# Attention over a sparse graph: pairs of row tiles that share one gather slot, and a new order of the instructions

## The chip, the cores and the metric

The kernel runs on one core of a Trainium2 chip. The metric is the device time of one launch in microseconds (us), the median of several runs. One profiled execution, taken by the hardware profiler, gives the rows that are quoted below; its clock begins at its first instruction.

## What is computed

Sixteen batches of 1024 rows of 512 numbers each; one adjacency matrix for all of them, in which row *i* has a one at each neighbour (itself among them).

```python
# x: (16, 1024, 512), adj: (1024, 1024), Wq, Wk, Wv: (512, 512)
h = jnp.maximum(_layernorm(x, axis=-1), 0.0)
q = (h @ Wq + bq).reshape(b, n, 8, 64)          # k and v alike
scores = jnp.einsum('bihd,bjhd->bhij', q, k) / jnp.sqrt(jnp.float32(64))
scores = scores + jnp.where(adj == 0, -1e9, 0.0)
weights = jax.nn.softmax(scores, axis=-1)
out = x + jnp.einsum('bhij,bjhd->bihd', weights, v).reshape(b, n, 512)
```

The number of neighbours differs much from row to row: a few rows have many, most have one to four. The kernel works with lists of neighbours and never forms the 1024 x 1024 scores.

## The kernel before

**Tiles, slots, units.** The rows are sorted by their number of neighbours and cut into eight tiles of 128 rows, tile 0 with the longest lists. `CAPS` = (11, 8, 6, 5, 4, 3, 3, 2) says how many neighbours a row of tile 0, 1, ..., 7 gets. A *slot* is one neighbour for each of the 128 rows of a tile: K and V of that neighbour, 128 x 1024 numbers, 512 KB. Together with a unit of 4 slots (tile "-1") for rows of tile 0 whose list is longer still, a batch has 46 slots. They are grouped into 14 *units* (`PARTS`: tile, first slot, count). A slot that a row does not need still is fetched and worked on (it points to a spare row, and its weight is taken out of the sums).

**The work of a batch.** PE projects K and V of the batch (`proj_kv`), tile by tile, from the transposed normalized rows (`flip` on PE, `unflip` copies them out on ACT); ACT or DVE takes K and V out of PSUM (`evict_kv`), SP stores them to DRAM (`store_kv`). When all eight tiles are stored, POOL fetches the slots with an indirect DMA each (`gather`); a tile's own rows come by a plain DMA on SP. The slots lie in a ring of `RING` = 23. Then for each unit: DVE multiplies K with the queries (`multiply`, line 1360, the queries lie in a PSUM bank), DVE sums over the 64 columns of each head (`score`, L1364), ACT takes exponents (`exponent`, L1368), ACT multiplies V by the weights, eight small instructions for a slot (`weigh_s`, L1394), or DVE with one (`weigh_v`, L1380), and DVE or POOL add the slots of the unit together (`fold`, L1399; `join`, L1406, adds one unit to another). Tile 0 and the pieces of long rows are added by PE (`add_up`, L1418). DVE forms the sums of weights (`row_sums`, `more`), POOL or DVE adds the result to x and POOL writes it out by an indirect DMA.

**Overlap.** PE projects K and V of batch *b*+1 while DVE, ACT and POOL work on the units of batch *b*; the queries of batch *b* (`queries`, names `pq_<batch>_<tile>`) are projected in between. Before batch 0 the program loads the adjacency matrix, sums it, ranks the rows by a comparison of keys (`keys`, `rank_of`, `ranks`), and builds the lists; K and V of batch 0 are projected meanwhile from x in its given order (names with `_first`).

**What sets the order.** Every engine runs its instructions in program order. That order comes from `PLACES`, a table of one number for each step of a batch (`PERIOD` is added for each batch): `Plan.ordered` sorts the steps of each engine by this number and holds a step back only until what it needs has been issued and its buffer is free in the order of `POOLS`. PSUM gives two banks to the queries (`'q': 2`), two to K and V, two to the transposes and two to the sums. So the queries of a tile can begin only after the multiplications with the queries two tiles earlier.

## Time and profile before

| | |
|---|---|
| three runs | 1610.32, 1606.07, 1604.77 us; median 1606.07 us |
| span of the profiled execution, first to last instruction | 1595.8 us (the median is 10.3 us above it) |
| busy | PE 97%, its weight loads 45%, DVE 96%, ACT 90%, POOL 79% |
| DMA | 531.55 MB in the whole span |
| phases | 0 to 95 us: lists, and K and V of batch 0; then units; K and V of the last batch end at 1496.8 us; end 1595.8 us |

The time of the profiled execution is not listed apart from its span; what lies around the span is taken as the 10.3 us between it and the median of the runs. A share of the span is an average over the phases; the rows below therefore cut the span into stretches of 100 us.

### The profile page before, as it was taken

How to read it: one execution, taken by the hardware profiler on the slowest of the kernel's cores; microseconds unless marked ns; L12 is line 12 of the kernel's file. 1: busy time of each engine (PE TensorE's matmuls, PEld its weight loads, DVE VectorE, ACT ScalarE, POOL GpSimd, SP SyncE). 2: the span in 40 equal slices, each digit the busy share in tenths (PEclk: the TensorE clock that was granted, in tenths of full speed). 3: DMA queues.
4: the chain of work that ended last, by engine and by line, in shares of the span. 5: the costliest groups of instructions: out<-in, count | busy, mean ns of one | idle time of the engine just before them, and what ended most of it. 6: DMA issues, size and time to landing. Idle time of an engine off the chain costs nothing.

```text
span 1595.8 us, 19282 instructions
## 1 busy us (share of the span) xinstructions
PE 1548.5 (97%) x4151; PEld 719.2 (45%) x4182; DVE 1532.9 (96%) x2105; ACT 1437.5 (90%) x5428; POOL 1257.0 (79%) x1185
## 2 busy tenths in 40 slices
PE   8999999999999999999999999999999999999877
PEld 4444444444444444444444444444444444444333
DVE  8879999999999999999999999999999999999997
ACT  4359989889999999999999999999999998998997
POOL 3767788887888888888888888888888878876775
PEclk9999999999999999999999999999999999999989
DMA  6498989998999999999999999999999999988994
GB/s 251 141 356 308 323 331 347 343 344 323 320 376 340 371 333 337 344 346 375 335 354 343 352 340 342 373 347 372 326 357 339 342 368 328 364 338 295 333 376 191
DMA packets 149875, 531.55 MB, mean 333 GB/s; under 512 B 19052, under 2 KB 19052, under 8 KB 149752
## 3 DMA queue, kind: packets, MB, share of 16 engines
q0 software_dynamic: 109840, 390.70, 67.2%
q1 hardware_dynamic: 39912, 139.56, 23.7%
q8 instruction: 35, 0.57, 0.1%
q14 instruction: 88, 0.72, 0.1%
HBM read 429.46 MB, written 100.72 MB: 332 GB/s over the span
## 4 chain that ended last, share of the span: by engine, by line
DVE 39%; PE 22%; ACT 12%; POOL 10%; issue 9%; DMA 7%; DVEq 0%; POOLq 0%; SPq 0%; ACTq 0%
DVE ring L1360 11%; DVE weights L1364 10%; ACT ring L1394 9%; DVE ring L1399 6%; DMA ring<-kv,index 6%; PE pk L1117 5%; PE pv L1117 5%; PE pq L1117 5%; POOL ring L1350 4%; DVE ring L1380 3%; DVE st L1071 2%; PE pv_first L1117 2%; PE pk_first L1117 2%; POOL ring L1399 2%; POOL x L1062 1%
## 5 line engine op out<-in xcount | busy, mean ns | idle before, releaser
L1394 ACT ACTIVATE ring<-ring,weights 128x64 f32<-128x64 f32 x4704 | 1154.6, 343 | 43.4 <-DVE weights L1373 42.4
L1350 POOL DMA_INDIRECT ring<-kv,index x608 | 618.0, 1016 | 185.5 <-issue 159.7
L1117 PE MATMUL pq<-wq,hT 128*128 128x512 f32 x1024 | 460.3, 592 | 0.8
L1117 PE MATMUL pv<-wv,hT 128*128 128x512 f32 x960 | 433.2, 594 | 3.5 <-ACT kvt L1135 3.3
L1117 PE MATMUL pk<-wk,hT 128*128 128x512 f32 x960 | 433.2, 594 | 1.9 <-ACT hT L1109 1.2
L1364 DVE TENSOR_REDUCE weights<-ring 128x32 f32<-128x2048 f32 (+2 forms) x224 | 422.2, 1890 | 0.9
L1360 DVE TENSOR_TENSOR ring<-ring,pq 128x1536 f32<-128x1536 f32 (+2 forms) x208 | 388.7, 1869 | 4.6 <-DMA ring<-kv,index 4.0
L1117 PEld LDWEIGHTS pq<-wq,hT 128*128 128x128 f32 x1024 | 194.5, 190 | 215.0 <-issue 211.1
L1117 PEld LDWEIGHTS pv<-wv,hT 128*128 128x128 f32 x960 | 182.1, 191 | 227.1 <-issue 216.4
L1117 PEld LDWEIGHTS pk<-wk,hT 128*128 128x128 f32 x960 | 182.7, 191 | 211.0 <-issue 200.6
L1399 DVE TENSOR_TENSOR ring<-ring 128x512 f32<-128x512 f32 (+1 forms) x301 | 253.0, 856 | 2.7 <-ACT ring L1394 2.1
L1471 POOL DMA_INDIRECT out_dram<-x,perm x128 | 151.3, 1182 | 38.1 <-issue 24.4
L1062 POOL DMA_INDIRECT x<-in_x_dram,perm x128 | 142.3, 1111 | 34.0 <-issue 27.6
L1399 POOL TENSOR_TENSOR ring<-ring 128x512 f32<-128x512 f32 x90 | 116.1, 1299 | 10.0 <-DVE ring L1399 8.3
L1380 DVE TENSOR_TENSOR ring<-ring,weights 128x512 f32<-128x512 f32 x143 | 105.8, 747 | 1.3 <-ACT weights L1368 1.0
L1097 ACT ACTIVATE h<-x,shift,rstd 128x512 f32<-128x512 f32 x120 | 94.0, 814 | 0.9 <-DVE shift L1087 0.9
L1468 POOL TENSOR_TENSOR x<-x,o 128x512 f32<-128x512 f32 x64 | 82.4, 1288 | 15.3 <-DVE o L1454 12.7
L1104 PEld LDWEIGHTS pht<-ident,h 128*128 128x128 f32 x512 | 61.9, 141 | 55.6 <-issue 47.8
L1368 ACT ACTIVATE weights<-weights 128x32 f32<-128x32 f32 (+2 forms) x224 | 48.8, 223 | 42.0 <-DVE weights L1364 41.2
L1071 DVE BATCH_NORM_STATS2 st<-x 128x6 f32<-128x512 f32 x120 | 81.2, 677 | 0.1
L1135 ACT COPY kvt<-pk 128x512 f32<-128x512 f32 x120 | 69.4, 578 | 7.8 <-PE pk L1117 7.8
L1104 PE MATMUL pht<-ident,h 128*128 128x128 f32 x512 | 72.7, 274 | 2.7 <-ACT h L1097 2.7
(240 smaller groups left out, 1088.0 us busy)
## 6 DMA issues: line engine op xcount, KB each, us to landing
ring<-kv SPq DMA_DIRECT2D x128, 512.0 KB, 6.7
kv<-kvt SPq DMA_DIRECT2D x120, 512.0 KB, 6.5
ring<-kv,index POOLq DMA_INDIRECT x608, 7.0
ring<-in_adj_dram SPq DMA_DIRECT2D x8, 512.0 KB, 8.2
x_first<-in_x_dram SPq DMA_DIRECT2D x8, 256.0 KB, 6.0
x<-in_x_dram,perm POOLq DMA_INDIRECT x128, 6.1
out_dram<-x,perm POOLq DMA_INDIRECT x128, 5.8
wk<-in_L_gnn_Wk_dram SPq DMA_DIRECT2D x1, 1024.0 KB
```

What stands on the lines that cost most here:

```text
L1062: nc.gpsimd.indirect_dma_start(out=X[n][:], out_offset=None, in_=x_rows, in_offset=on(ap=perm[:, t : t + 1], axis=0), element_offset=b * N * D
L1071: nc.vector.bn_stats(st, X[n])
L1097: nc.scalar.activation(HN[n], X[n], AF.Relu, bias=shift, scale=scale)
L1104: nc.tensor.transpose(PH[n][:, c, :], hn[:, ts(c, P)], ident)
L1117: nc.tensor.matmul(pt, HT[n][:, c, :], W[name][:, c, :], start=(apart and c == 0), stop=(n != -NT and c == DC - 1))
L1350: nc.gpsimd.indirect_dma_start(out=G[i][:, s].rearrange("p j d -> p (j d)"), out_offset=None, in_=KV[b % len(KV)][:], in_offset=on(ap=inde ...
L1360: nc.vector.tensor_tensor(k, k, Q[b, t][:, None, :].to_broadcast([P, count, D]), ALU.mult)
L1364: nc.vector.tensor_reduce(weights[:, w, :], heads(G[i][:, :count, 0, :]), AX.X, ALU.add)
L1380: nc.vector.tensor_tensor(v, v, own.to_broadcast([P, n, H, HD]), ALU.mult)
L1394: nc.scalar.activation(v[:, h, :], v[:, h, :], AF.Identity, scale=weights[:, c + s, h : h + 1])
L1399: engine.tensor_tensor(v[:, 0:n], v[:, 0:n], v[:, first : first + n], ALU.add)
L1471: nc.gpsimd.indirect_dma_start(out=out_rows[t], out_offset=on(ap=perm[:, t : t + 1], axis=0), in_=X.pop(b * NT + TILES.index(t))[:], in_of ...
```

## The change

Tiles 2 and 3 give up their own last slot and share one: rows 0 to 63 of the shared slot serve the last neighbour of tile 2's rows, rows 64 to 127 that of tile 3's. Tiles 0 and 1 do the same, with rows 0 to 95 for tile 0 and rows 96 to 127 for tile 1. For this the rows of tiles 3 and 1 lie in reverse order in their tile, so that their longest lists stand at the high rows. A batch has 44 slots and 13 units; the ring has 22.

A shared slot needs a tile of mixed queries (`mix`, two copies on ACT for each pair: rows from one bank and from the other; the copy of tile 0's queries that was there, `copy_q`, is one of them), a multiplication of its own (`multiply_m`), a split of its weights (`halves`, two small copies on ACT), and two additions, one for each side (`fold_m` and `join_m` on DVE; in the last batch `add_m` on PE). `ranks` gets seven more small DVE instructions, which turn the order of tiles 1 and 3. Which slots DVE weighs is now written for each unit; nine per batch, as before. All numbers of `PLACES` are new.

```diff
-    3: ((3, 0, 3), (3, 3, 2)),
-    2: ((2, 0, 3), (2, 3, 3)),
+    3: ((3, 0, 5),),
+    2: ((2, 0, 3), (2, 3, 2)),
     1: ((1, 0, 4), (1, 4, 4)),
-    0: ((0, 0, 4), (-1, 0, 4), (0, 4, 4), (0, 8, 3)),
+    0: ((0, 0, 4), (-1, 0, 4), (0, 4, 4), (0, 8, 2)),
 }
+SHARED = {3: (2, 64), 1: (0, 96)}
...
-BY_VECTOR = {2: 1, 3: 0, 4: 1}
-ONE_MORE = ((2, 0),)
+BY_VECTOR = {(7, 0): 1, (4, 0): 1, (3, 0): 1, (2, 3): 1, (1, 0): 1, (1, 4): 1, (0, 0): 1, (-1, 0): 1, (0, 4): 1}
...
-PERIOD = 95.290021
+PERIOD = 93.3
...
-        queries=(102.781, 109.589, 125.334, 130.63, 135.829, 151.822, 160.48, 186.198, 199.518,),
+        queries=(104.758, 106.455, 110.927, 120.802, 128.186, 137.177, 154.399, 157.941, 178.55,),
...
-POOLS = {'x': 16, 'h': 2, 'pht': 2, 'hT': 11, 'pkv': 2, 'kvt': 4, 'q': 2, 'q0': 1, 'acc': 2, 'o': 1}
-RING = 23
+POOLS = {'x': 16, 'h': 2, 'pht': 2, 'hT': 11, 'pkv': 2, 'kvt': 4, 'q': 2, 'q0': 1, 'qm': 1, 'acc': 2, 'o': 1}
+RING = 22
...
+                elif t in SHARED or t in LOW:
+                    add(("mix", b, t), "ACT", [("queries", b, t)], [q, mixed(b, t)])
...
+            add(("multiply_m", k), "DVE", [slots[m], of_low, ("mix", b, t)], [mixed(b, t)])
+            add(("score", k), "DVE", [("multiply", k), ("multiply_m", k)])
...
+            nc.vector.scalar_tensor_tensor(mirror, tile_of, float(P), rank, op0=ALU.mult, op1=ALU.subtract)
...
+            nc.vector.tensor_tensor(rank, rank, mirror, ALU.add)
+            nc.vector.tensor_copy(rank_i, rank)
...
+            rows = dict(sides(high))[t]
+            nc.scalar.copy(QM[b, high][rows, :], Q[b, t][rows, :])
...
+        def multiply_m(i):
+            k = GM[i][:, 0, :]
+            nc.vector.tensor_tensor(k, k, QM[i // NU, UNITS[i % NU][0]], ALU.mult)
+
+        def halves(i):
+            high = UNITS[i % NU][0]
+            for t, rows in sides(high):
+                nc.scalar.copy(weights[rows, part_col[t], :], weights[rows, shared_col[high], :])
...
+        def fold_m(i):
+            rows = sides(UNITS[i % NU][0])[1][1]
+            v = G[i][rows, 0, 1, :]
+            nc.vector.tensor_tensor(v, v, GM[i][rows, 1, :], ALU.add)
+
+        def join_m(i):
+            low, rows = sides(UNITS[i % NU][0])[0]
+            v = G[i // NU * NU + parts_of(low)[0]][rows, 0, 1, :]
+            nc.vector.tensor_tensor(v, v, GM.pop(i)[rows, 1, :], ALU.add)
```

Counted over the whole program, gathers fall from 608 to 576 and the small weighing instructions of ACT from 4704 to 4448. On DVE the multiplications of 1536 columns go from 96 to 64, those of 1024 from 32 to 48, 32 of 512 are new, and the additions of 512 columns (`fold` and `join` before, with `fold_m` and `join_m` after) go from 286 to 271. On POOL the folds go from 90 to 105. PE's multiplications are the same in number but for one. The numbers of `PLACES` move instructions in three places that matter below.

SP, first instructions of the program, before (loads of x, of the biases, of the weights and of blocks of the adjacency matrix; `ring` is where biases and adjacency land):

```order
L1060 DMA x_first_0_151<-in_x_dram 128x512
L1060 DMA x_first_1_168<-in_x_dram 128x512
L951 DMA ring_104<-in_L0_gnn_bk_dram 3x512
L951 DMA ring_104<-in_L0_gnn_bv_dram 3x512
L951 DMA ring_104<-in_L0_gnn_bq_dram 3x512
L938 DMA wk_111<-in_L0_gnn_Wk_dram 128x4x512
L935 DMA ring_104<-in_adj_dram 128x1024
```

and after, at the same place:

```order
L1054 DMA ring_107<-in_adj_dram 128x1024
L1190 DMA x_first_2_163<-in_x_dram 128x512
L1070 DMA ring_107<-in_L0_gnn_bv_dram 3x512
L1190 DMA x_first_1_166<-in_x_dram 128x512
L1190 DMA x_first_0_170<-in_x_dram 128x512
L1054 DMA ring_107<-in_adj_dram 128x1024
L1070 DMA ring_107<-in_L0_gnn_bq_dram 3x512
L1057 DMA wk_114<-in_L0_gnn_Wk_dram 128x4x512
L1070 DMA ring_107<-in_L0_gnn_bk_dram 3x512
```

The weights of K, which stood behind two tiles of x (0.5 MB), now stand behind three tiles of x and two blocks of the adjacency matrix (1.75 MB).

PE, queries of tiles 4, 3 and 2 of batch 8, before (`chosen` adds the bias, `pk_9_5` is a projection of the next batch, `pht` a transpose):

```order
L1115 MATMUL pq_8_4_7388<-bias_parts_141,chosen_121 128x512
L1117 MATMUL pq_8_4_7388<-wq_113,hT_8_4_6583 128x512 x4
L1115 LDWEIGHTS chosen_121
L1115 MATMUL pq_8_3_7434<-bias_parts_141,chosen_121 128x512
L1117 MATMUL pq_8_3_7434<-wq_113,hT_8_3_6757 128x512 x4
L1115 LDWEIGHTS chosen_121
L1115 MATMUL pk_9_5_7466<-bias_parts_141,chosen_121 128x512
L1117 MATMUL pk_9_5_7466<-wk_111,hT_9_5_7380 128x512 x4
L1104 MATMUL pht_9_3_7476<-ident_114,h_9_3_7384 128x128 x4
L1115 LDWEIGHTS chosen_121
L1115 MATMUL pq_8_2_7514<-bias_parts_141,chosen_121 128x512
```

and after:

```order
L1245 MATMUL pq_8_4_7272<-bias_parts_144,chosen_124 128x512
L1247 MATMUL pq_8_4_7272<-wq_116,hT_8_4_6616 128x512 x4
L1245 LDWEIGHTS chosen_124
L1245 MATMUL pq_8_3_7290<-bias_parts_144,chosen_124 128x512
L1247 MATMUL pq_8_3_7290<-wq_116,hT_8_3_6654 128x512 x4
L1245 LDWEIGHTS chosen_124
L1245 MATMUL pq_8_2_7305<-bias_parts_144,chosen_124 128x512
L1247 MATMUL pq_8_2_7305<-wq_116,hT_8_2_6808 128x512 x4
L1247 MATMUL pv_9_5_7319<-wv_115,hT_9_5_7266 128x512 x4
```

Between the queries of tiles 3 and 2 stood a projection of K and four transposes; now nothing stands there, and the projections of the next batch follow behind.

DVE, in batch 8, around the multiplication with the queries of tile 3, before (`weights` holds the scores and weights of all slots):

```order
L1360 TENSOR_TENSOR ring_104<-ring_104,pq_8_3_7434 128x3x512
L1440 TENSOR_REDUCE sums_8_7301<-weights_140 128x8
L1444 RECIPROCAL inv_8_4_7442<-sums_8_7301 128x8
L1373 TENSOR_TENSOR weights_140<-weights_140,inv_8_4_7442 128x32
L1380 TENSOR_TENSOR ring_104<-ring_104,weights_140 128x512
L1360 TENSOR_TENSOR ring_104<-ring_104,pq_8_3_7434 128x2x512
L1364 TENSOR_REDUCE weights_140<-ring_104 128x24
L1364 TENSOR_REDUCE weights_140<-ring_104 128x16
```

and after:

```order
L1523 TENSOR_TENSOR ring_107<-ring_107,pq_8_3_7290 128x4x512
L1630 TENSOR_REDUCE sums_8_7234<-weights_143 128x8
L1634 RECIPROCAL inv_8_4_7386<-sums_8_7234 128x8
L1527 TENSOR_TENSOR ring_107<-ring_107,qm_8_3_7349 128x512
L1545 TENSOR_TENSOR weights_143<-weights_143,inv_8_4_7386 128x32
L1263 TENSOR_TENSOR kvt_9_5_7417<-pv_9_5_7319,bias_rows_148 128x512
L1536 TENSOR_REDUCE weights_143<-ring_107 128x40
```

The two units of tile 3 (3 and 2 slots, two scores) have become one multiplication of 4 slots, the one with the mixed queries `qm`, and one score of 5 slots.

## Rows read from the trace of the kernel before

**Rows 1.** Busy time of the engines, from the profile's page.
```profile
PE 1548.5 (97%) x4151; PEld 719.2 (45%) x4182; DVE 1532.9 (96%) x2105; ACT 1437.5 (90%) x5428; POOL 1257.0 (79%) x1185
```

**Rows 2.** Stretches: length, busy PE, PEld, DVE, ACT, POOL; PEclk, DMA share, GB/s.
```profile
0.00:100.00 100.00, 92.29 (x278) 45.88 (x282) 80.79 (x235) 44.18 (x72) 62.02 (x82) 0.98 0.63 225
100.00:200.00 100.00, 98.33 (x272) 45.84 (x273) 97.90 (x138) 90.83 (x342) 72.01 (x68) 1.00 0.92 327
200.00:300.00 100.00, 97.55 (x257) 44.48 (x257) 98.77 (x130) 90.55 (x348) 81.50 (x75) 1.00 0.93 335
300.00:400.00 100.00, 95.49 (x261) 44.38 (x261) 96.04 (x123) 89.58 (x341) 78.78 (x72) 1.00 0.92 340
...
1000.00:1100.00 100.00, 99.89 (x274) 46.89 (x275) 98.75 (x130) 95.81 (x365) 82.74 (x79) 1.00 0.97 359
...
1400.00:1500.00 100.00, 96.50 (x253) 44.43 (x254) 95.75 (x112) 88.30 (x340) 70.36 (x67) 0.98 0.88 322
1500.00:1595.00 95.00, 71.88 (x164) 30.14 (x163) 85.84 (x102) 82.99 (x351) 63.07 (x61) 0.89 0.77 288
```

**Rows 3.** Timeline of PE in batch 8: start, length, instruction.
```profile
850.56 0.38 PE L1115 MATMUL pq<-bias_parts,chosen 128*128 128x512 bf16 x1
...
858.94 0.38 PE L1115 MATMUL pq<-bias_parts,chosen 128*128 128x512 bf16 x1
859.16 3.60 PE L1117 MATMUL pq<-wq,hT 128*128 128x512 f32 x8
862.59 0.38 PE L1115 MATMUL pk<-bias_parts,chosen 128*128 128x512 bf16 x1
...
879.36 0.38 PE L1115 MATMUL pq<-bias_parts,chosen 128*128 128x512 bf16 x1
```

**Rows 4.** Timeline of PE, one step of batches 8 and 12.
```profile
947.47 0.28 PE L1433 MATMUL p_more<-more,owner_t 128*128 128x8 f32 x2
...
1319.51 0.28 PE L1433 MATMUL p_more<-more,owner_t 128*128 128x8 f32 x2
```

**Rows 5.** What PE waited for, 100 to 420 us: total, times, longest.
```profile
PE pk L1115 <- ACT kvt L1135: 2.0, 2, 1.4
PE pk L1115 <- DVE kvt L1133: 1.4, 1, 1.4
```

**Rows 6.** What PE waited for, 420 to 1497 us.
```profile
PE pv L1117 <- ACT kvt L1135: 2.6, 1, 2.6
PE pv L1115 <- ACT kvt L1135: 1.5, 2, 0.8
```

**Rows 7.** Timeline of DVE in batch 8: its first multiplication, and tile 4's.
```profile
857.04 1.22 DVE L1360 TENSOR_TENSOR ring<-ring,pq 128x1024 f32<-128x1024 f32 x1
...
872.78 2.28 DVE L1360 TENSOR_TENSOR ring<-ring,pq 128x2048 f32<-128x2048 f32 x1
```

**Rows 8.** Groups of instructions by shape: busy us, mean ns; idle before.
```profile
L1364 DVE TENSOR_REDUCE weights<-ring 128x24 f32<-128x1536 f32 x96 | 166.9, 1739 | 0.5
L1360 DVE TENSOR_TENSOR ring<-ring,pq 128x1536 f32<-128x1536 f32 x96 | 167.6, 1746 | 2.3 <-DMA ring<-kv,index 2.3
L1399 DVE TENSOR_TENSOR ring<-ring 128x512 f32<-128x512 f32 x211 | 140.6, 687 | 1.2 <-ACT ring L1394 0.7
```

**Rows 9.** Groups of ACT and POOL on the page: busy us, mean ns; idle before.
```profile
L1394 ACT ACTIVATE ring<-ring,weights 128x64 f32<-128x64 f32 x4704 | 1154.6, 343 | 43.4 <-DVE weights L1373 42.4
L1350 POOL DMA_INDIRECT ring<-kv,index x608 | 618.0, 1016 | 185.5 <-issue 159.7
```

**Rows 10.** The start: PE's timeline.
```profile
9.97 3.60 PE L1117 MATMUL pk_first<-wk,hT_first 128*128 128x512 f32 x8
...
87.15 0.66 PE L1104 MATMUL pht<-ident,h 128*128 128x128 f32 x4 [1.55 <-ACT h L1097]
```

**Rows 11.** A stretch of the start, columns as in rows 2.
```profile
5.00:15.00 10.00, 8.61 (x25) 3.88 (x24) 5.78 (x19) 5.43 (x9) 4.71 (x9) 1.00 1.02 399
```

**Rows 12.** The end: PE's last projection of K and V gives way to queries.
```profile
1496.78 0.38 PE L1115 MATMUL pq<-bias_parts,chosen 128*128 128x512 bf16 x1
```

More of the change, by code (lines that the diff above doesn't have):

```diff
@@ L146 @@
[L146 to L154 removed]
+        load_x=(61.723, 62.777, 65.014, 67.869, 68.549, 72.226, 74.997, 75.728,),
@@ L468, in ordered @@
                 new = [use for use in self.ops[i][3] if use not in has]
-                if all(k in made for k in known[i]) and all(given[use[0]] == at[use] for use in new):
+                if all(k in made for k in known[i]) and all(
+                    given[use[0]] == at[use] and not left.get(before.get(use), 0) for use in new
+                ):
                     ready.append((place[i], i, new))
@@ L474, in ordered @@
                 given[use[0]] += 1
+            for use in self.ops[i][3]:
+                left[use] -= 1
             made.add(i)
@@ L627, in planned @@
         add(("exponent", k), "ACT", [("score", k)])
+        if m is not None:
+            add(("halves", k), "ACT", [("exponent", k)])
         weights = ("exponent", k)
@@ L710, in planned, with readers_of @@
     return plan
+def readers_of(plan, k, name):
+    b, u = divmod(k, NU)
+    t = UNITS[u][0]
+    homes = [t]
+    if name == "halves":
+        homes.append(SHARED[t][0])
+    found = [("more", b) if home < 0 else ("row_sums", b, home) for home in homes]
+    if name == "score":
+        found += [("halves", k), ("share", k), ("weigh_v", k), ("weigh_p", k)] + [("weigh_s", k, s) for s in range(UNITS[u][2])]
+    return [key for key in found if key in plan.number]
 def ring_of(B):
```

798 lines of the change are left out of this document (465 added, 333 removed), and 36 rows, old and new, of the table gather.

## The prediction

> **What bounds the kernel now.** I read the busy shares first. PE is busy 97% of the span, DVE 96%, ACT 90%, POOL 79% [rows 1]. Two engines within one per cent of each other can't be told apart by their shares, so the next view is the one by stretches of 100 us [rows 2]: in the middle (1000 to 1100) PE is busy 99.89% and DVE 98.75%. The reader should see that PE leaves 0.11 us of 100, and that PE's share is lower at both ends of the program: 92.29 in the first stretch, 98.33, 97.55 and 95.49 in the next three, 96.50 in the one before the last, and 71.88 of 95 us at the end.
>
> The third view is PE's timeline, which says whether "busy" is work. A projection of queries is one bias step and eight half-steps: it begins at 858.94, its main part at 859.16, the next projection at 862.59 [rows 3]. So a projection takes 862.59 - 859.16 = 3.43 us and its bias 0.22, with nothing between them. The fourth view is the period: the same step of batches 8 and 12 stands at 947.47 and 1319.51 [rows 4], 372.04 us for four batches, 93.01 us each. DVE and ACT are nearly full, yet the batch lasts exactly as long as PE's list of instructions. **PE is the bound in the middle; DVE and ACT are late only at the start of the pipeline and at its end.**
>
> What PE waits for agrees: between 100 and 420 us it is the eviction of K and V by ACT (2.0 us) and DVE (1.4 us), with smaller ones behind them [rows 5], and from 420 to 1497 us almost only ACT's evictions, 2.6 and 1.5 us [rows 6].
>
> The Trainium skill speaks against reading it so: "Perfetto Trace Analysis", section "Identifying the Most-Contended Engine", says that the busy share of matmuls is no good measure of how near TensorE is to its limit, and that the share of weight loads is the better one; that share is 45% here, which would make DVE the bound and give the time of the second rival below. The starts 3.43 us apart in rows 3 disagree with such headroom.
>
> **The change part by part.**
>
> *DVE.* One slot has 512 columns in the multiplication and in the score. 1536 columns take 1.746 and 1.739 us [rows 8], so a slot costs 0.58 + 0.58 = 1.16 us, and two slots less are 2.3 us a batch. The additions of 512 columns go from 286 to 271, 15 x 0.687 = 10 us or 0.6 us a batch [rows 8]. Together some 2.8 us a batch, 45 us in all, of 1532.9 busy [rows 1]. A lone 512-column addition takes 0.687 against 0.582 for a third of a multiplication, so an instruction costs about 0.1 us beside its columns; there are 16 multiplications more and 16 scores less, which cancel.
>
> *ACT.* 256 weighing instructions go, at 1154.6/4704 = 0.245 us [rows 9]: -63 us. 48 more copies of 512 columns come, about 0.58 us each if they cost what a full copy costs (an estimate from a third of rows 8's 1.746), +28 us, and 64 small `halves`, which at the price of a weighing instruction are +16 us. Sum about -19 us, 1.2 a batch.
>
> *POOL.* 32 gathers less, 1.016 us and about 0.26 of issue each (159.7 us of issue over 608) [rows 9]: -41 us; 15 folds more, which at the price of a gather each are +19 us.
>
> *PE.* Nothing: the same projections, one sum more. So in the middle none of this moves the end. 93.01 us a batch stays [rows 4], and what DVE, ACT and POOL save turns into idle time there. The saving counts only where PE waits for them, and behind PE's last projection.
>
> *Ramp, 100 to 400 us.* PE is idle 1.67 + 2.45 + 4.51 = 8.6 us [rows 2], of which 0.3 stays by the measure of the middle. Its causes are evictions that stand behind other work on ACT and DVE [rows 5]. Three batches with 2.8 us less on DVE and 1.2 less on ACT are 12 us of relief, more than the waits; but the order is another one, and some evictions will again stand badly. Bounds 0 and -8; I take **-6**.
>
> *Late waits, 400 to 1500 us.* 3.5 us in the stretch before the last [rows 2], mostly ACT's 2.6 and part of its 1.5 [rows 6], and about 2 us before. Bounds 0 and -5.5; I take **-4**, near the upper end, since these few stand where particular instructions met and not in each batch.
>
> *The end.* From PE's last projection of K and V at 1496.78 [rows 12] to 1595.8 are 99 us; DVE is busy 85.84 of the last 95 us and ACT 82.99 [rows 2], so here DVE and ACT set the time. The last batch has 2.8 us less on DVE and 1.2 less on ACT, and DVE comes to it with less left over from the batch before, worth at most another 2.8. The order of the units in it is new, which can cost as much. Bounds +2 and -6; I take **-3.5**.
>
> *The start.* Here the change loses. The first K projection starts at 9.97 [rows 10], once the weights of K have landed. Before, 1.5 MB had to land up to them, now 2.75 MB: 1.25 MB more at 399 GB/s [rows 11] is 3.1 us. ACT now has one more pass over a tile and one over the biases ahead of the first tile, about 1 us by the estimate for a copy, so the first projection starts near 14. The ranking gets seven small DVE steps on its one chain, each between the 0.1 us above and a whole addition's 0.687: 0.7 to 4.8 us, of which I take 1.5, since they have few columns. Against it, PE waits later anyway for rows of batch 1 (1.55 us at 87.15) [rows 10], and a late start of PE is partly taken up there. Bounds 0 (all of it taken up) and +8 (both delays, and a lower clock behind a longer idle time: the last stretch, where PE is idle for a quarter, shows 0.89 [rows 2]); I take **+4**.
>
> *New waits in the middle.* PE now projects the queries of tiles 4, 3 and 2 without anything between. Two banks hold queries, so tile 2's wait for the multiplication with tile 4's. Before, tile 4's ended at 872.78 + 2.28 = 875.06 [rows 7], and tile 2's queries began at 879.36 [rows 3], 4.3 us later. In the new order, six projections (6 x 3.65), two sums, eight transposes and a sum of weights (1.9 us together) lie between the start of tile 7's queries and the wish for tile 2's: 23.8 us. DVE's first multiplication came 857.04 - 850.56 = 6.5 us behind that start [rows 3, 7], and DVE's new list from there to the end of tile 4's multiplication adds up to 15.6 us by the durations of its kinds, against 18.0 before. 23.8 - 22.1 = 1.7 us of room: just enough. Cost **0**; what it costs when the room is gone is the third rival.
>
> Sum: -6 - 4 - 3.5 + 4 = -9.5. Span 1595.8 - 9.5 = 1586.3; with the 10.3 us that the median of the runs has above the span, **1596.5 us**. The ends of the terms give 1606.07 - 19.5 + 0 = 1586.5 and 1606.07 + 2 + 8 = 1616.
>
> **The rivals.** A difference below about 0.3% (1601.3 to 1610.9 us) can't be told from no change.
>
> *The waits stay.* The new order puts new evictions behind other work, ramp and late waits give back 3 us instead of 10, and the start costs 4: 1606 - 3 - 2 + 4 = 1605 us, no change. For it: these waits come from single meetings of instructions in the order, and the order is wholly new; it gives the same result if PE's list simply stays the time. Against it: DVE and ACT have less to do in every batch. Chance 0.24.
>
> *DVE is the bound after all.* Then DVE's 45 us go through: 1606 - 45 + 4 = 1565 us. For it DVE's 98.75% in the middle [rows 2]; against it the 93.01 us that equal PE's list. Chance 0.05. The rule of the Trainium skill in "Perfetto Trace Analysis", above, would make this the forecast.
>
> *Queries too close together: slower.* If DVE runs later against PE than I worked out, tile 2's queries wait in every batch, and the queries of tiles 1 and 0 wait also for the copies `mix`, which stand on ACT behind eight to 24 weighing instructions of 0.245 us [rows 9], 2 to 6 us. PE gets that time back nowhere, since it is full. With 3.2 us of lateness, 1.5 us over the room of 1.7, it is 1.5 x 14 = 21 us, and without the ramp's gain 1606 + 21 - 9.5 + 2 = 1620 us. It decides from about 1 us a batch. For it: the room is less than half of what it was, and one engine more stands in the chain. Against it: DVE's lists are shorter, which makes it earlier. Chance 0.13.
>
> That the change does not do what it says is out: the instructions of the changed program show 576 gathers and 44 slots.
>
> **How the numbers follow.** Forecast 1596.5 with 0.58; of that, its own range is 1587 to 1604, with 0.02 of its weight faster by less than 0.3% counted under "same". "Waits stay" 0.24, DVE 0.05, slower 0.13. Faster by over 0.3%: 0.56 + 0.05 = 0.61. Within 0.3%: 0.02 + 0.24 = 0.26. Slower: 0.13. The range of 8 in 10 runs from 1583 (the lower end of the terms, 1586.5, and some of the way to DVE's case) to 1616 (their upper end), which leaves out the DVE case and the worse half of the slower one.
>
> **What would show it.** In the trace of the changed kernel: the step of rows 4 still 93.0 us apart in the middle, with PE at 99.9% and DVE some 3 points lower; the first K projection near 14 us; PE idle between 100 and 400 us about 3 us, not 8.6; the last projection of K and V ending near 1491, and some 95.5 us from there to the end; DVE busy near 1488, ACT near 1418. The forecast is wrong if the period is under 93 us (DVE had been the bound), if PE shows a wait before queries that repeats each batch (third rival), or if the idle time between 100 and 400 us is as before. It is right only by accident if the end or the start moved by other amounts than stated.

## The result and the profile after

The changed kernel takes **1690.18 us** (median of 4 runs, 1686.53 to 1692.29) against 1606.23 (1604.77 to 1610.32): a ratio of 1.052, 95% interval 1.050 to 1.054. The forecast was 1596.5 with a range to 1616. It is wrong in size and in sign. The profiled run took 1691.75 us, its span 1690.0: what lies around a span is 1.7 us here and 1.7 to 2.1 in every run below, not the 10.3 us that were set on top of the forecast's span. The execution profiled before, with its span of 1595.8, therefore took some 1597.5 us, about 9 less than the median of its kernel. So the two spans differ by 94.2 us, while the medians differ by 84.0.

Busy time of the engines, from the page of the changed kernel:
```profile
PE 1580.6 (94%) x4182; PEld 727.4 (43%) x4182; DVE 1566.3 (93%) x2104; ACT 1423.7 (84%) x5268; POOL 1290.2 (76%) x1168
```
Beside [rows 1], ACT fell by 14 us, much as forecast. DVE has one instruction less and should have lost 45 us; it is busy 33 us *more*. POOL should have lost 22, gaps of issue included, and has 33 us more of busy time. So instructions became longer.

Stretches of the changed kernel; columns as in [rows 2]:
```profile
0.00:100.00 100.00, 81.83 (x233) 39.73 (x234) 72.02 (x215) 34.72 (x57) 56.29 (x74) 0.91 0.53 184
100.00:200.00 100.00, 90.27 (x254) 43.21 (x252) 83.09 (x141) 72.30 (x250) 64.68 (x61) 0.97 0.79 285
200.00:300.00 100.00, 91.15 (x241) 41.33 (x240) 97.47 (x117) 87.59 (x331) 71.86 (x65) 0.98 0.85 294
300.00:400.00 100.00, 96.06 (x252) 44.03 (x251) 92.23 (x119) 88.32 (x331) 80.44 (x73) 0.98 0.89 326
...
1000.00:1100.00 100.00, 96.83 (x262) 44.89 (x261) 96.35 (x122) 91.35 (x345) 81.06 (x72) 1.00 0.90 323
...
1600.00:1690.00 90.00, 63.49 (x132) 25.54 (x132) 73.27 (x86) 69.78 (x293) 54.70 (x51) 0.85 0.68 251
```
In the middle PE was busy 99.89 us of 100 and is now 96.83: the pipeline no longer runs at PE's pace. The ramp got worse instead of better, and the last stretch is emptier on every engine.

Where the 94.2 us of span went follows from PE's last K or V step of each batch, read from its timeline:

| end of K/V of batch | 0 | 1 | 3 | 4 | 14 | 15 | span |
|---|---|---|---|---|---|---|---|
| before | 75.2 | 176.4 | 370.0 | 464.8 | 1399.0 | 1496.8 | 1595.8 |
| changed | 84.4 | 201.1 | 405.0 | 503.4 | 1483.3 | 1580.2 | 1690.0 |

The start costs 9.2 us, batches 1 to 3 cost 25.8 more, batches 4 to 15 48.4 more, the end (batch 15 to the last instruction) 10.8 more. From batch 4 to 14 a batch takes (1483.3 - 503.4)/10 = 98.0 us, against 93.4.

What PE waited for from 420 to 1590 us (total, times, longest):
```profile
PE pv L1245 <- DVE kvt L1263: 29.3, 11, 3.2
PE pk L1245 <- ACT kvt L1265: 5.1, 6, 2.0
...
PE pq L1245 <- DVE ring L1523: 0.3, 1, 0.3
```
One wait a batch (11 in the stretch) has taken the place of [rows 6]: V's projection waits until DVE has evicted the V before it. The queries of tiles 4, 3 and 2, which the third rival feared, wait 0.3 us in the whole stretch. PE's timeline in one of these batches:
```profile
883.91 0.38 PE L1245 MATMUL pk<-bias_parts,chosen 128*128 128x512 bf16 x1 [1.26 <-ACT kvt L1265]
...
891.33 0.58 PE L1245 MATMUL pv<-bias_parts,chosen 128*128 128x512 bf16 x1 [3.17 <-DVE kvt L1263]
891.71 4.85 PE L1247 MATMUL pv<-wv,hT 128*128 128x512 f32 x8
```
Two gaps, 4.4 us, and then a projection of 4.85 us in place of 3.60, because the clock granted from 891.7 to 896.6 us is 0.74 on average, against 1.00 from 884 to 888: together 5.7 us of the 99 that this batch lasts. Why DVE is late stands in its own timeline just ahead of that eviction, and in POOL's. First DVE:
```profile
881.52 1.80 DVE L1552 TENSOR_TENSOR ring<-ring,weights 128x512 f32<-128x512 f32 x1
...
888.76 1.91 DVE L1552 TENSOR_TENSOR ring<-ring,weights 128x512 f32<-128x512 f32 x1
890.60 0.68 DVE L1263 TENSOR_TENSOR kvt<-pv,bias_rows 128x512 f32<-128x512 f32 x1
```
Then POOL:
```profile
881.47 1.29 POOL L1660 TENSOR_TENSOR x<-x,o 128x512 f32<-128x512 f32 x1
...
885.69 1.83 POOL L1663 DMA_INDIRECT out_dram<-x,perm  x1 [0.30 <-issue]
...
888.84 1.28 POOL L1571 TENSOR_TENSOR ring<-ring 128x512 f32<-128x512 f32 x1
```
`weigh_v` of one slot, 512 columns, takes 1.80 and 1.91 us; where nothing meets it, it takes 0.68. Both times an addition of POOL (the residual of line 1660, the fold of line 1571, 1.28 us each) lies over it. DVE's groups by shape show that this is a matter of kinds (busy us, mean ns; idle before):
```profile
L1571 DVE TENSOR_TENSOR ring<-ring 128x1024 f32<-128x1024 f32 x90 | 128.9, 1432 | 11.8 <-ACT ring L1566 9.7 <-DVE ring L1552 0.5
L1552 DVE TENSOR_TENSOR ring<-ring,weights 128x512 f32<-128x512 f32 x143 | 125.8, 881 | 0.9 <-ACT weights L1540 0.5
L1571 DVE TENSOR_TENSOR ring<-ring 128x512 f32<-128x512 f32 x151 | 116.8, 774 | 0.8
L1523 DVE TENSOR_TENSOR ring<-ring,pq 128x1536 f32<-128x1536 f32 x64 | 111.7, 1745 | 6.9 <-PE pq L1247 5.5 <-DMA ring<-kv,index 0.8 <-ACT qm L1500 0.5
L1536 DVE TENSOR_REDUCE weights<-ring 128x24 f32<-128x1536 f32 x48 | 83.5, 1741 | 0.0
...
L1596 DVE TENSOR_TENSOR ring<-ring 128x512 f32<-128x512 f32 x60 | 50.4, 840 | 0.5
```
The multiplication with queries (one operand from PSUM) and the score (one operand) have the times of [rows 8] to a few ns. The additions and `weigh_v`, whose two operands both lie in SBUF, have grown: 0.774 against 0.687 for 512 columns. Summed over DVE's kinds, what instructions last beyond the lower quartile of their kind is 101 us, against 31 before. Of the instructions with two operands of 512 or 1024 columns in SBUF, 63 are stretched by over a quarter, against 12 before; the 63 last 1.2 us longer on average, and each overlaps an addition of POOL. How a stretched one ends shows what the hold is: the 48 of 512 columns end 0.55 to 0.56 us after POOL's addition has ended and the 15 of 1024 columns 1.09 us after it, although 30 of the 63 began ahead of that addition. So nearly all of their work is done after it; the two exclude one another. Five meetings recur: `fold` of unit (4, 0) with residual 5, `join` with POOL's fold of unit (-1, 0), `weigh_v` of unit (1, 4) with residual 2 and `weigh_v` of unit (0, 0) with POOL's fold of unit (1, 0) in 8 to 10 of the middle batches each, `fold` of unit (6, 0) with residual 0 in every second one.

The hold works the other way too. POOL's gathers on the page, against [rows 9]:
```profile
L1511 POOL DMA_INDIRECT ring<-kv,index x576 | 629.6, 1093 | 198.9 <-issue 128.6
```
32 gathers fewer take 12 us more, 1.093 us each against 1.016. 134 of them last over 1.3 times the usual 0.94 us, against 60 before, and every one of the 134 overlaps a DVE instruction with two operands in SBUF. So do 216 of the other 442, which are not stretched that far: a meeting is needed, and does not always cost.

### The profile page after: what moved, and what is told of

It reads as the page before. It is cut to its first block, busy times and chain, and to the rows that moved or that the text cites. A ratio compares the mean times of both kernels' runs of the same rounds, so it can differ in the third digit from the quotient of the medians.

```text
span 1690.0 us, 19109 instructions
## 1 busy us (share of the span) xinstructions
PE 1580.6 (94%) x4182; PEld 727.4 (43%) x4182; DVE 1566.3 (93%) x2104; ACT 1423.7 (84%) x5268; POOL 1290.2 (76%) x1168
## 4 chain that ended last, share of the span: by engine, by line
DVE 28%; PE 22%; POOL 14%; ACT 13%; issue 11%; DMA 11%; another core or an unknown queue 1%; DVEq 0%; POOLq 0%; SPq 0%
ACT ring L1566 11%; DMA ring<-kv,index 8%; DVE ring L1523 7%; PE pv L1247 7%; DVE weights L1536 7%; POOL ring L1511 7%; PE pq L1247 5%; PE pk L1247 5%; DVE ring L1571 4%; POOL x L1660 2%; DVE st L1201 2%; POOL ring L1571 2%; POOL out_dram L1663 1%; PE pk_first L1247 1%; DVE ring L1552 1%
## 5 line engine op out<-in xcount | busy, mean ns | idle before, releaser
L1566 ACT ACTIVATE ring<-ring,weights 128x64 f32<-128x64 f32 x4448 | 1096.3, 338 | 62.6 <-DVE weights L1545 60.2
L1511 POOL DMA_INDIRECT ring<-kv,index x576 | 629.6, 1093 | 198.9 <-issue 128.6
L1247 PE MATMUL pv<-wv,hT 128*128 128x512 f32 x960 | 446.5, 609 | 3.6 <-ACT kvt L1265 3.4
L1536 DVE TENSOR_REDUCE weights<-ring 128x32 f32<-128x2048 f32 (+3 forms) x208 | 402.8, 1943 | 0.5
L1523 DVE TENSOR_TENSOR ring<-ring,pq 128x2048 f32<-128x2048 f32 (+2 forms) x192 | 351.8, 1833 | 24.6 <-DMA ring<-kv,index 14.6
L1663 POOL DMA_INDIRECT out_dram<-x,perm x128 | 143.8, 1123 | 37.1 <-issue 30.9
L1571 POOL TENSOR_TENSOR ring<-ring 128x512 f32<-128x512 f32 x105 | 134.5, 1282 | 18.7 <-ACT ring L1566 12.7
L1552 DVE TENSOR_TENSOR ring<-ring,weights 128x512 f32<-128x512 f32 x143 | 125.8, 881 | 0.9 <-ACT weights L1540 0.5
L1540 ACT ACTIVATE weights<-weights 128x32 f32<-128x32 f32 (+3 forms) x208 | 46.0, 222 | 58.5 <-DVE weights L1536 47.0
L1239 ACT COPY hT<-pht 128x512 f32<-128x512 f32 x128 | 73.4, 576 | 9.6 <-issue 4.8
```

The lines of the kernel that those rows point to most:

```text
L1247: nc.tensor.matmul(pt, HT[n][:, c, :], W[name][:, c, :], start=(apart and c == 0), stop=(n != -NT and c == DC - 1))
L1511: nc.gpsimd.indirect_dma_start(out=G[i][:, s].rearrange("p j d -> p (j d)"), out_offset=None, in_=KV[b % len(KV)][:], in_offset=on(ap=inde ...
L1523: nc.vector.tensor_tensor(k, k, Q[b, t][:, None, :].to_broadcast([P, count, D]), ALU.mult)
L1536: nc.vector.tensor_reduce(weights[:, w, :], heads(G[i][:, :count, 0, :]), AX.X, ALU.add)
L1552: nc.vector.tensor_tensor(v, v, own.to_broadcast([P, n, H, HD]), ALU.mult)
L1566: nc.scalar.activation(v[:, h, :], v[:, h, :], AF.Identity, scale=weights[:, c + s, h : h + 1])
```

## The experiments

Each time below is of one run, beside one of the kernel before on the same chip (1604.0, 1619.1 and 1596.8 us on three chips, 1599.8 and 1599.4 on a fourth; the changed kernel itself 1694.9 on the second, 1680.1 on the third). So whole times are compared within a chip, and else the length of a batch, taken from 4 to 14. Theory **L**: DVE and POOL hold one another up over SBUF, and that makes the batch. Theory **O**: PE's wait is a badly placed eviction, and the stretch is harmless.

**Taking the meetings away.** `thin_after` and `thin_before` shorten POOL's additions in either kernel, from 512 to 16 columns; the other columns are left out:
```diff
-            engine.tensor_tensor(v[:, 0:n], v[:, 0:n], v[:, first : first + n], ALU.add)
+            cols = slice(0, 16 if engine is nc.gpsimd else D)
+            engine.tensor_tensor(v[:, 0:n, cols], v[:, 0:n, cols], v[:, first : first + n, cols], ALU.add)
...
-            (nc.vector if residual_by_vector(b, B, t) else nc.gpsimd).tensor_tensor(rows, rows, add, ALU.add)
+                nc.gpsimd.tensor_tensor(rows[:, :16], rows[:, :16], add[:, :16], ALU.add)
```


> The changed kernel with POOL's additions (folds and residuals) cut from 512 to 16 columns; the other 496 columns of those additions are left out. Theory L (a DVE addition or weighing with two operands in SBUF stands still while POOL runs an addition): in the changed kernel 91 such DVE instructions last 1.1 to 1.3 us longer than their kind, 8 to 10 times in 11 middle batches at the same five places; with short POOL additions these vanish, the batch falls from about 98 to 93 to 94 us, and the time from 1690 to 1625 to 1645 us. Theory O (the new order lets PE wait for DVE's eviction of V, 3.2 us a batch, because it stands behind the multiplication with the passed-on queries): the order is untouched, so the batch stays at 97 us or more and the time above 1670 us.

> The kernel before with the same cut of POOL's additions to 16 of 512 columns, as a control. Theory L: it has only about 23 such long instructions in 16 batches, so little is to be had: 1590 to 1606 us. If short POOL additions by themselves saved time (POOL earlier at its gathers), it would fall as far as the changed kernel does, by 45 us or more.

1609.4 and 1578.0 us. Stretch from 500 to 1300 us of `thin_after` (length, busy PE, PEld, DVE, ACT, POOL):
```profile
500.00:1300.00 800.00, 799.46 (x2165) 373.35 (x2172) 764.56 (x1019) 752.42 (x2824) 536.03 (x605) 1.00 0.93 340
```
PE is busy 799.46 us of 800, a batch is 93.2 us, and DVE is busy 1483.3 us in all, near the 1488 of the prediction. The old order also gains, 26 us, more than the 1.2 us for each of its 12 stretched instructions. The stretched gathers are not what makes the batch long: 121 last as long here, where the batch is 93.2 us. Without meetings the new order still ends 1607.6 - 1576.2 = 31.4 us of span behind the old: 8.1 by batch 0, 14.9 in batches 1 to 3, nothing from 4 to 14, and the rest at the end.

This shortens POOL's work too, from 79.5 to 62.4 us a batch, so `write_only` keeps POOL longer occupied (72.2 us) and lets it only write:
```diff
-            engine.tensor_tensor(v[:, 0:n], v[:, 0:n], v[:, first : first + n], ALU.add)
+                nc.gpsimd.memset(v[:, 0:n], 0.0)
+                nc.gpsimd.memset(v[:, first : first + n], 0.0)
```
(and the same for the residual).

> The changed kernel with each addition of POOL (folds, residuals) replaced by two fills with zero, of its target and of its other operand; the additions themselves are left out. A fill of 456 columns took 0.483 us, so POOL is busy about 1.1 us in each such place, as with an addition (1.28), but it reads nothing from SBUF. Theory L in its narrow form (DVE's second operand waits for POOL's reading): the long DVE instructions vanish, the batch is 93 to 94 us, the time 1610 to 1635 us. If POOL's own time is what delays the batch (its gathers stand behind the additions), or if any access of POOL stops DVE: 97 us or more a batch, above 1665 us.

1626.2 us, 68.6 under the changed kernel on that chip; a batch is 93.2 us, and the excess of DVE's durations falls from 101 us to 18:
```profile
500.00:1300.00 800.00, 799.33 (x2158) 372.69 (x2166) 765.62 (x1019) 751.06 (x2827) 620.04 (x724) 1.00 0.94 339
```
A fill of 512 columns takes 0.54 us, two of them nearly an addition, and DVE is not held. So POOL's writing does not hold DVE; what is left is that POOL's *reading* of SBUF meets DVE's second operand. Here the Trainium skill agrees: "SBUF — State Buffer", section "Who interferes with whom", says that DVE and GpSimd share a port pair held by one of them for a whole instruction, and that a DVE instruction with two SBUF inputs contends with a GpSimd instruction that reads SBUF and not with one that only writes it. It does not agree that such DVE instructions leave the issue of DMAs alone, as the same section infers: the 134 stretched gathers above speak against that.

`thin_folds` shortens only the folds, which take part in two of the five meetings.

> The changed kernel with the folds on POOL cut to 16 of 512 columns; the residual additions stay whole. Of the five meetings of a batch two are with a fold (join, weigh_v of unit 0) and three with a residual. If each meeting costs alike (about 1 us of lateness, 5 us a batch for five), a batch lasts 93 + 3 = 96 us and the run takes about 1650 us. If only the sum over a bound counts (DVE's list of 92.9 us plus the stretch against PE's 93.0), the same, since DVE has nothing to spare. If the folds in front of PE's sums are what matters, 93 to 94 us and under 1630 us.

1646.0 us and a batch of 95.6 us:
```profile
500.00:1300.00 800.00, 783.02 (x2106) 362.59 (x2115) 779.34 (x988) 731.58 (x2737) 612.81 (x590) 1.00 0.92 332
```
With three of the five meetings left, 2.4 of 4.8 us are left over the 93.2 without any. POOL is busy 73.2 us a batch here, about as in `write_only`, whose batch lost nothing: so these 2.4 us are the meetings and not POOL's load.

**Moving the work instead of cutting it.** `evict_early` puts the V eviction that PE waited for ahead of the work in front of it, in batches 3 to 12:
```diff
+MOVED = (
+    (lambda b: ("evict_kv", (b + 1) * NT + TILES.index(1), 1), lambda b: ("score", b * NU + unit_of(0, 0))),
+)
...
+                    result[i] = result[k] + 0.0005
```


> The changed kernel with one step moved in batches 3 to 12: DVE's eviction of V of tile 1 of the next batch goes from behind the multiplication with the passed-on queries and a weighing to right behind the score of tile 0's first unit, some 7 us earlier. Theory O: PE's wait of 3.2 us and the slow clock behind it (1.2 us) go, 10 x 4.4 us: 1640 to 1650 us. Theory L: DVE's own list is as long as before and paces the batch; 1675 to 1690 us, and PE waits elsewhere.

1675.0 us; a batch still takes 97.5. That wait shrinks from 29.3 us to 3.7, and another comes: from 420 to 1480 us PE's sums wait nine times, 20.6 us in all, for POOL's folds. **Theory O falls**: the eviction is where the lateness shows, not where it arises. `apart` moves four of the DVE instructions that met additions, and `apart_more` seven (same mechanism, other rows in `MOVED`).

> The changed kernel with four DVE instructions moved in batches 3 to 12, each behind the next score or multiplication with PSUM: the weighing of unit (1,4), the weighing of (0,0), the join of (0,0), the first fold of (4,0). These are the four that last 1.1 us longer in 8 to 10 of 11 middle batches while POOL adds. Theory L: 4 x 1.1 us x 10 batches less, 1640 to 1655 us, unless the additions meet others instead. Theory O: two of the four stand ahead of the late eviction, so at most 2.3 us a batch, 1665 to 1690 us, with PE's wait for the eviction halved but there.

> The changed kernel with seven DVE instructions moved in batches 3 to 12: the weighings of (1,4) and (0,0) as in the first such run, and the three that met POOL's additions there instead (weighings of (4,0) and (3,0), fold of (0,8)), with the join of (0,0) and the first fold of (4,0) behind them, each next to an instruction that reads only one operand from SBUF. Theory L: DVE's list without meetings is about 93 us a batch, so with most of them gone the batch is 93 to 95.5 us, 25 to 45 us below the changed kernel on the same chip. If DVE were held by something else, or if each such move only makes it meet another addition: 97 us a batch, at most 15 us below it.

`apart`: 1675.4 us and 97.4 us a batch. The moved instructions met other additions: three new pairs, each in nine or ten batches, and the excess fell only from 101 to 84 us. `apart_more` did cut it, to 64 us, but took 1686.8 us, 6.8 *more* than the changed kernel on that chip, with 98.4 us a batch. Its middle:
```profile
500.00:1300.00 800.00, 767.58 (x2042) 353.57 (x2050) 738.59 (x965) 715.80 (x2685) 642.36 (x568) 0.99 0.89 319
```
And what DVE waited for from 420 to 1480 us:
```profile
DVE shift L1233 <- POOL rstd L1229: 33.9, 19, 2.4
DVE ring L1592 <- POOL ring L1587: 9.9, 8, 1.2
```
DVE is busy only 738.59/800 x 98.4 = 90.9 us a batch, less than PE's 93, and waits for POOL. So DVE's stretched time alone can't be what sets the batch here, and L needed a second half.

**DVE's lateness or POOL's?** `late_dve` is `thin_after` with about 1.1 us of extra DVE work (two sums that nobody reads) behind each of the five instructions; `late_pool` is `write_only` with three fills for two; `late_both` has both. `late_pool_before` makes the edit of `late_pool` in the old order; `late_dve_before` is `thin_before` with such sums behind two instructions, the fold of unit (4, 0) and the join of unit (0, 0), which brings DVE's total to that of `late_dve`.
```diff
+                for k, cols in enumerate((D, D // 2)):
+                    unread = small.tile([P, 1], F32, tag="unread", name=f"unread_{i}_{k}")
+                    nc.vector.tensor_reduce(unread, src[:, :cols], AX.X, ALU.add)
```


> The changed kernel with POOL's additions cut to 16 of 512 columns (as in thin_after, where a batch lasts 93.0 us, so no engine holds another up), and behind each of the five DVE instructions that met an addition in the changed kernel two more DVE instructions that sum 512 and 256 columns from SBUF into a number nobody reads, about 1.0 us together, in batches 1 to 14. So DVE is as late as in the changed kernel, at the same places, while POOL is not. If DVE's lateness alone makes the period (theory V), a batch lasts 97 to 99 us and the run takes 1665 to 1690 us. If POOL's own lateness is needed (theory P), it stays at 93 to 94 and the run under 1630 us.

> The changed kernel with POOL's additions replaced by zero fills, three of 540 ns for each instead of the two of write_only (1.6 us in place of an addition's 1.28): POOL is later than in the changed kernel, and nothing holds DVE. If POOL's time alone makes the period (theory P), a batch lasts over 96 us and the run takes over 1660 us. If DVE's lateness does (theory V), it stays at 93.0 and the run takes 1620 to 1635 us, as write_only did.

> Both of the above at once: three zero fills for each of POOL's additions, and the two additional sums behind the five DVE instructions. Theory V: as late_dve, 97 to 99 us a batch. Theory P: as late_pool. If neither alone does it but both do, it is over 97 us here and under 95 in the other two.

> The kernel before with POOL's additions cut to 16 of 512 columns (as in thin_before: 93.0 us a batch, DVE busy 91.2 of it), and behind the fold of unit (4, 0) and the join of unit (0, 0) two more DVE sums of 511 and 255 columns each, about 2.2 us a batch, in batches 1 to 14. That brings DVE's busy time to 93.4 us a batch, as in late_dve, whose batch lasted 96.3. If any order of this program pays about 3 us of idle time once DVE's list is as long as PE's (theory G), a batch lasts about 96 us here and the run takes over 1615 us. If the old order holds DVE full and only the new one does not (theory N), it lasts 93.4 to 94.5 us and the run takes 1583 to 1600 us.

> The kernel before with POOL's additions replaced by three zero fills of 540 ns each, the edit of late_pool, whose batch lasted 96.7 us with DVE busy 88.9 of it. If the old order has room for a later POOL and the new one has none (theory N), a batch lasts 93.0 to 93.5 us here and the run takes 1578 to 1590 us. If a later POOL costs any order of this program the same (theory G), it lasts about 96 us and the run takes over 1615 us.

The runs took 1648.4, 1656.5, 1665.9, 1593.6 and 1620.8 us (the kernel before: 1599.8 and 1599.4). Busy time per batch is the stretch's busy share times the batch:

| kernel | batch, us | DVE busy in it | POOL busy in it |
|---|---|---|---|
| before | 93.4 | 91.4 | 77.6 |
| changed | 98.0 | 94.8 | 79.5 |
| thin_after | 93.2 | 89.0 | 62.4 |
| thin_folds | 95.6 | 93.1 | 73.2 |
| write_only | 93.2 | 89.2 | 72.2 |
| late_dve | 96.3 | 93.3 | 62.9 |
| late_pool | 96.9 | 89.1 | 81.3 |
| late_both | 96.9 | 93.4 | 79.7 |
| late_dve_before | 94.1 | 93.1 | 63.2 |
| late_pool_before | 96.1 | 91.0 | 79.8 |

The rows behind four of these, in the order `late_dve`,
```profile
500.00:1300.00 800.00, 780.86 (x2088) 361.64 (x2096) 775.65 (x1066) 725.26 (x2713) 522.46 (x586) 0.99 0.91 329
```
`late_pool`,
```profile
500.00:1300.00 800.00, 775.27 (x2077) 358.85 (x2085) 735.22 (x984) 722.86 (x2703) 671.02 (x810) 1.00 0.91 327
```
`late_dve_before`,
```profile
500.00:1300.00 800.00, 793.37 (x2126) 367.69 (x2141) 791.59 (x1045) 755.14 (x2894) 537.84 (x607) 1.00 0.95 347
```
and `late_pool_before`:
```profile
500.00:1300.00 800.00, 782.11 (x2082) 361.43 (x2097) 757.76 (x995) 740.82 (x2840) 664.63 (x810) 1.00 0.93 338
```
Three things follow. First, each lateness alone makes 3.1 to 3.7 of the 4.8 us by which a batch of the changed kernel exceeds `thin_after`, DVE's at 93.3 us of work (the changed kernel: 94.8) and POOL's at 81.3 (79.5). The two do not add: `late_both` is no longer than `late_pool`. Second, POOL has little room in *either* order: at 80 us of busy time the old order pays too (96.1), and the old order ran close below that, at 77.6. Of the 135 us in which POOL is idle between 500 and 1300 us of `late_pool_before`, 96 are gaps of about 0.3 us between instructions, so 80% busy is near full here. Third, at 93.1 us of DVE work the old order takes 94.1 us, keeping DVE 99% busy (791.59 of 800), and the new one takes 96.3. That points to the order, but the added work stands at two places in the one and at five in the other, and the two were not separated.

**The start.** `loads_first` brings the weights of K, the biases and the first tiles ahead of the adjacency rows; `start_order` also moves one `degree`, `parts_at` and one `stats` behind the first tiles' work; `both_orders` is that with the moves of `apart_more`.
```diff
-        load_w=(-22.638, 27.467, 32.983,),
-        load_b=(-20.612, -72.455, -25.768,),
+        load_w=(-98.0, 27.467, 32.983,),
+        load_b=(-98.4, -98.3, -98.2,),
```


> The changed kernel with only its first loads in the old order: two tiles of x, the biases and the weights of K ahead of the adjacency matrix. Theory S (the late start is the weights' late landing and the half clock behind PE's 5 us of waiting): K and V of batch 0 end at 76 to 80 us instead of 84, and the whole is 4 to 8 us shorter. Rival: the adjacency matrix, now later, holds back the ranking and the lists by 3 us, and the end of batch 1 is where it was, within 2 us.

> The changed kernel with its first steps in another order: two tiles of x, biases and weights of K loaded first, and on DVE the statistics of those two tiles and the masks for the biases ahead of the first block of the adjacency matrix. Theory D (PE's late start is DVE's order: the statistics stand behind a degree that waits for the adjacency matrix): the first K projection begins at 9 to 12 us instead of 14.8, K and V of batch 0 end at 76 to 80 us instead of 84, and the end of batch 1 moves by as much. Rival: the lists set the start of batch 0's units, so the end of batch 1 stays within 2 us of the changed kernel's.

> Both edits together, the moved DVE instructions of batches 3 to 12 and the start. If the two causes are apart from each other, it wins the sum of the two within 5 us: 30 to 50 us below the changed kernel on this chip by theories L and D, still 20 us or more above the kernel before, since the ramp of batches 1 to 3 (15 us with POOL's additions cut) and the end (8 to 11 us) are untouched.

`loads_first`: 1698.4 us, and batch 0 ends at 88.2 in place of 84.4; the statistics of the first tile stand on DVE behind `degree`, which now waits 7.4 us for the adjacency. So the order of the loads alone is not the loss. `start_order`: 1673.4 us, 6.6 under the changed kernel on that chip; the first projection comes at 11.2 us, yet batch 0 ends at 82.5 against 82.9, since the projection then waits 2.65 us for the biases and runs slowly. So four microseconds gained at the first instruction gave 0.4 at the end of batch 0. `both_orders`: 1681.4 us, 1.3 over the changed kernel.

`old_order` runs the new instructions, with 44 slots, at the places that the old kernel's trace shows for the same steps (the table of places exchanged, the new steps set beside their nearest).

> The shared slots in the order of the kernel before: every step that both kernels have stands where the trace of the kernel before had it, the new steps stand behind what they need; the last batch keeps the changed kernel's order among its units. All work is done. Theory L (the shared slots are sound, the new order makes DVE and POOL meet): few long DVE instructions, a batch of 93 to 95 us, 1600 to 1630 us. Rival T (the shared slots themselves cost: mixed queries on ACT in the chain, one chain more between the pairs of tiles): above 97 us a batch, 1660 us or more.

1747.7 us, some 101 us a batch. DVE waits for POOL's folds, 420 to 1480 us:
```profile
DVE ring L1504 <- POOL ring L1499: 35.2, 10, 3.8
```
An order carried over by hand is worse than either, so it doesn't tell what the shared slots are worth under a good order. Batch 0 ends at 76.5, though, near the old 75.2: the loss at the start comes with the new places, not with the shared slots.

`after_again` and `after_third` are the changed kernel itself, for comparison on two of the chips.

> The changed kernel itself, once more, beside the next three on one chip. Both theories: 1685 to 1693 us as before, if the 11 us that the two reordered kernels won in batch 1 (116.7 us before, 105.4 in both), which their edit does not touch, came from the edit in some way; about 1677 us, if that was a disturbance of the first profiled run or of its chip.

> The changed kernel once more, as the measure for the next three on this chip: 1675 to 1695 us, batch 1 of 105 us if the chip shows none of the stalls in which several engines wait at 77 to 120 us without a releaser in the trace, 117 us if it does.

They show 98.0 and 97.9 us a batch. Batch 1 takes 117.8 us in the one and 107.0 in the other. In the slower case, and in the first profile of the changed kernel, ACT stands still twice, in that profile for 9.2 us up to 89 us and for 7.5 up to 111 us, and PE behind it. ACT's waits from 76 to 125 us in that first profile:
```profile
ACT h L1227 <- issue: 17.2, 3, 7.5
...
ACT kvt_first L1265 <- remote: 9.2, 1, 9.2
```
Neither names an engine that it waited for; it was not found what held it.

## Why the prediction was wrong

*The bound of the middle* was read rightly for a program without meetings: with them gone the period is 93.2 us, with PE busy 799.46 of 800. DVE as the bound, the second rival and the reading of the Trainium skill's "Perfetto Trace Analysis", did not give its 1565 us either: DVE's list became longer, not shorter.

*The step that failed is the price of DVE's and POOL's instructions: count times mean duration, with no term for what one engine does to the other.* [rows 8] gave 0.687 us for an addition. That mean already held stretched ones, and the shape it was used for has 0.683 without meetings and 0.774 in the changed kernel. What an addition costs depended on what POOL does at that moment, and the change moves every instruction against every other. For DVE -45 us were forecast. Without POOL's additions its busy time falls from 1511.2 to 1483.3, 28 us; the stretch rises by 61, from 21.7 (1532.9 - 1511.2) to 83.0 (1566.3 - 1483.3), where 0 stood. That `thin_after` comes near the forecast 1488 is partly luck, since the forecast started from a total that held the old stretch. The trace of before had the sign of it: a `weigh_v` of 1.94 us among ones at 0.69. A mean hides that; the longest beside the shortest of one shape shows it.

*New waits in the middle: 0 forecast.* Measured: 4.6 us a batch, 48 us in all. The third rival had the sign and, with 1620 us, a sixth of the size (14 of 84 us), but the wrong place: queries in a row cost nothing, V's eviction waits behind DVE's stretched list. It also weighed only DVE's lists as sums. "DVE's lists are shorter, which makes it earlier" was its counter-argument, and is the failed step once more.

*Ramp: -6 forecast, +25.8 measured* in batches 1 to 3. Of that 14.9 come without any meeting (thin against thin), so they belong to the new order of the ramp; some 10 are ACT's standstill, which not every chip shows (`after_third`, where it is missing, has +15.3). "Relief of DVE" was no argument for a ramp whose instructions were all placed anew.

*The end: -3.5 forecast, +10.8 measured.* What DVE waited for from 1580 to 1690 us:
```profile
DVE ring L1523 <- DMA ring<-kv,index: 9.2, 3, 4.3
DVE ring L1523 <- PE pq L1247: 1.9, 2, 1.7
```
And PE, in the same stretch:
```profile
PE acc L1610 <- ACT ring L1566: 10.2, 3, 5.1
PE acc L1610 <- POOL ring L1571: 9.0, 1, 9.0
```
Before, DVE waited 0.3 us for gathers there. The last batch's gathers now come late on POOL, and DVE, 85.84 of 95 us busy in [rows 2], is busy 73.27 of 90. The term took DVE and ACT as the bound of the tail and left POOL out. Thin additions leave most of the loss, so it is mainly the order's; which place makes it was not tried.

*The start: +4 forecast, +9.2 measured.* The first projection was expected near 14 us and came at 15.49; then it lost 2.5 us more to the clock, which the term named only in its upper bound:
```profile
13.60 1.12 PE L1234 MATMUL pht_first<-ident,h_first 128*128 128x128 f32 x4 [6.08 <-ACT h_first L1227]
15.49 6.13 PE L1247 MATMUL pk_first<-wk,hT_first 128*128 128x512 f32 x8 [0.78 <-ACT hT_first L1239]
```
PE stood idle for 6.08 us and the eight half-steps behind it take 6.13 us, against 3.60 in [rows 10], so for much of it the lower of the two levels, 1.2 GHz, was granted: 0.50 from 13.5 to 15.5 us and 0.60 from 15.5 to 21.6, where the old kernel has 1.00 from 9.9 to 13.6. The first 100 us have 0.91 on average, 0.98 in [rows 2].

*Late waits: -4 forecast.* Drowned by the new wait. *ACT and the counts of instructions* came out as worked out: 1423.7 (1418 forecast).

In sum, the parts are clearest in the spans without the standstill: `after_third` has 1678.4 us, 82.6 over the profile of before. Of these, 7.6 fall to the start, 15.3 to batches 1 to 3, 48.6 to batches 4 to 15 and 11.1 to the end. With POOL's additions cut in both orders the same parts are 8.1, 14.9, -0.2 and 8.6 us, 31.4 together: that is the new order at the start, in the ramp and at the end. The other 51, nearly all in batches 4 to 15, come and go with POOL's additions (profiles from different chips, which differ by some microseconds). How they divide between DVE's hold and POOL's own load is shown only in part: the three meetings left in `thin_folds` are worth 2.4 us a batch and DVE's lateness without any of POOL's 3.1, of 4.8. What stays open: which places of the ramp and the end make those 31; what holds ACT near 90 us on some chips; and whether the shared slots would win under an order searched with the meetings in its costs. That they could is only argued: DVE's list is 89.0 us a batch with them and 91.2 without (both with thin additions), but PE's 93.0 is the period of both, so there is no gain to be had in the middle.

## What to carry to other kernels

Before pricing a reordering, look at the spread of durations within one shape. If it is wide, find what overlaps the long ones, and treat the two engines' instructions of those kinds as excluding one another; here the additions that met made a batch 98.0 us long in place of 93.2. An engine at 80% busy whose gaps are issue time had no slack here, and where every engine has only a few microseconds of room in 93, moving the instruction that is seen to wait did not help: the wait came back elsewhere. A saving on an engine that is not the bound buys nothing, while the new order that comes with it can cost much.

## What the runs showed of the hardware

A DVE instruction of 0.68 us (512 columns) with both operands in SBUF takes 1.5 to 2.5 us when most of an addition of 1.28 us on POOL lies over it, and one of 1.21 us (1024 columns) takes 1.9 to 2.9. It ends a fixed time after POOL's addition, 0.55 to 0.56 us and 1.09 us, also where it began first (30 of 63 cases). In six other meetings it is POOL's addition that lasts longer, 1.4 to 1.8 us, and DVE keeps its time. A DVE instruction with an operand from PSUM, or with a single operand, keeps its time: the 49 multiplications of 2048 columns that overlap an addition for over 0.2 us have a mean of 2.277 us, and the 29 that overlap none have the same. Zero fills by POOL do not do this (0.54 us for 512 columns, DVE's excess 18 us in place of 101). POOL's issue of an indirect DMA, 0.94 us, takes 1.2 to 2.0 us, once 3.2, in 134 of 576 cases, and all 134 meet such a DVE instruction. And in the old kernel, too, cutting POOL's additions was worth 26 us, which no share of busy time had shown.
